# Identity transposes on TensorE during the first loads, a later place for pair 1's x transposes, and a later load of one block of the second weights, in a two-layer graph kernel

## The chip, the core and the metric

The kernel runs on one core of a Trainium2 chip. A core has five engines that run their own instruction streams and wait for each other through semaphores: TensorE (PE in the profile, with its weight loads as PEld), VectorE (DVE), ScalarE (ACT), GpSimd (POOL) and SyncE (SP). Transfers between HBM and on-chip memory are issued here from the queues of SP and ACT (SPq and ACTq) and carried by 16 DMA engines. The metric is the device time of one execution in microseconds (us); lower is better.

## The reference, cut to what matters

128 graphs of 128 nodes with 512 features each pass through two layers. In both, the result is added to the input and normalised over the features.

```python
# layer 0: attention over the neighbours, 8 heads of 64 units
feats = einsum('bnf,hfu->bhnu', X, W)
e_self, e_neigh = einsum('bhnu,hu->bhn', feats, a_self), einsum('bhnu,hu->bhn', feats, a_neigh)
dense = leaky_relu(e_self[..., :, None] + e_neigh[..., None, :], 0.2) + NEG_BIG * (1 - A)
out   = relu(einsum('bhij,bhju->bhiu', softmax(dense), feats) + b)
x = layernorm(x + out)

# layer 1: two hypergraph convolutions with a layer norm between them
H, w = (adj != 0), first row of adj
conv(x, W) = Dn * (H @ (Be * (H.T @ (x @ W.T)))) + bias      # Dn = 1/(H @ w), Be = 1/column sums of H
h = layer_norm(relu(conv(x, W1)), gamma, beta)
x = layernorm(x + conv(h, W2) + x)
```

## The kernel before

The graphs are taken in 64 pairs. Each pair runs through some ninety small steps: loads, transposes of x, features (a product with `w0_sb`), attention scores, masks, exponentials, transposes and weighted sums, the first normalisation, the propagator product, the hidden product with `w1_sb`, the output product with `w2_sb`, the last normalisation, the store. From pair 2 on, the products use sums of matrix blocks (seven products in place of eight), so that the weights need four extra sums of blocks each. Pairs 0 and 1 use plain products for the features (`plain_features`, lines 516 to 527) and transposes on TensorE in place of transposes on VectorE, because they run before everything else is ready.

The order of instructions is written out by hand. Every step has a time in a list (`todo`, lines 1140 to 1232): a step of pair p with lag l has the time (p + l) * 38.6 plus its own; the tables `todo` and `first` give special times for the start. The list is sorted by this time, and each engine's instructions are emitted in that order. The times are only keys for sorting: what runs when is decided by semaphores, and each engine and each DMA-issuing queue works strictly in its order. Line numbers below are those of the code before the change.

The steps of the start, in the order of their keys:

- Before the list: the input loads on SP and ACT (lines 177 to 189): the vectors `an_bc` and `as_bc`, four blocks of the first weights (`w0_raw`, `load_first`), x of pairs 0 and 1 (`load_rows`, line 120), adjacency rows. POOL writes the identity `ident` (line 206) that TensorE's transposes need.
- 11.1 and 12.0 `prepare_first` (line 228): for each of the four weight blocks a copy on ACT (L230), a product with `as_bc` on VectorE and with `an_bc` on POOL (L234), and two reductions on VectorE (L238). A block can be used by the features after its reductions.
- 11.4 `x_transpose_first` for pair 0 (line 393): eight transposes of x on TensorE into the banks `px` (L397). 11.5 `x_transpose_out`: two copies to `xT` on ACT (L405). `xT` has a single buffer, so that pair 1's copies wait until pair 0's features have been computed.
- 12.1 `load_weights` with `w2_blocks`: four loads of 512 KB of the second weights, issued on ACT's queue (L141).
- 12.5 `plain_features` 0 of pair 0, **12.55 `x_transpose_first` of pair 1**, 12.6 `plain_features` 1 of pair 0: TensorE (L523 and L397). A call of `plain_features` uses two weight blocks with four matmuls each, which the profile lists as eight records each.
- 12.65 `adj_transpose_first` (L410), 12.9 `nodes` (L360 to L369, VectorE), 13.0 `plain_features_out` (L533: copies of the features to `ft`, two on ACT and two on VectorE for pair 0), 13.05 `prepare_vectors`: one transpose on TensorE (L256) and its copy on ACT (L257), 13.1 the first copy to pair 1's `xT` on ACT.
- 13.5 `spread_rows` of pair 0: VectorE transposes `rows` (L542), and four small DMAs write them to `rd` in HBM, two issued by SP and two by ACT (L550). 13.8 the second copy to pair 1's `xT` on ACT.
- 14.0 `neighbours` of pair 0: two loads of 512 KB that spread `rd` to `nb`, one on SP and one on ACT (L570). 14.05 two blocks of the first hidden weights (`w1_blocks`) on ACT, and at 15.46 the other two on SP.
- 14.46 `edges`, 14.5 `plain_features` 0 of pair 1, 14.55 `propagator`, 14.6 `plain_features` 1 of pair 1, 16.0 `prepare_output` (lines 272 to 279: 32 matmuls `pv` over the four blocks of `w2_blocks`, in their order), then at 73 to 79 masks on POOL (L589), leaky ReLU on ACT (L605), maxima on VectorE (L611), exponentials on ACT (L619), the transposes `pet` on TensorE (L651), and the weighted sums `pav` (L677).

PSUM is used as eight banks of one pool: `bank(name)` takes the next, and a tile waits for the release of the one that had its bank.

Of the kernel before, what the change touches and what calls it, by code (L numbers as in the profile page):

```python
# [20 lines left out]
def kernel(  # L21
# [45 lines left out]
    nc = tc.nc  # L67
    G, N, F = x.shape
    P = 128
    DH = w1t.shape[1]  # L70
    H = 8
    U = F // H
    KF = F // P
    KH = DH // P
    HALF = 512
    QU = HALF // 2
# [12 lines left out]
    def bank(name):  # L89
        return psum.tile([P, HALF], F32, tag="bank", name=name)  # L90
# [95 lines left out]
    for i, ap in enumerate((gamma, beta, b1)):  # L186
# [7 lines left out]
    w2_blocks = ((w2_sb[:, 0, :, :QU], 0, 0), (w2_12, 0, 1), (w2_sb[:, 1, :, :QU], 1, 0),  # L194
                 (w2_sb[:, 2, :, :QU], 1, 1))
# [8 lines left out]

    ident = const.tile([P, P], F32, name="ident")
    make_identity(nc, ident)
    mhalf = const.tile([P, 2], F32, name="mhalf")
    nc.gpsimd.memset(mhalf, -0.5)

# [712 lines left out]
    def weigh(s, i, to, start):  # L922
# [3 lines left out]
          QU, 1, until=LAST)  # L926
# [197 lines left out]
    for t, fn, *args in (  # L1124
# [14 lines left out]
    T = 38.6  # L1139
    todo = [  # L1140
        (11.1, prepare_first, (0,)), (12.0, prepare_first, (1,)), (15.45, prepare_first_sums, ()),
        (12.1, load_weights, (nc.scalar, w2_blocks, w2t, DH // 2, QU)),
        (13.05, prepare_vectors, ()),
        (14.05, load_weights, (nc.scalar, w1_blocks[:2], w1t, F // 2, HALF)),
        (12.95, load_first_row, (1,)),
# [46 lines left out]

    for p, time, fn, *args in (
        (0, 11.4, x_transpose_first), (0, 11.5, x_transpose_out, 0), (0, 11.5, x_transpose_out, 1),
        (0, 12.5, plain_features, 0), (1, 12.55, x_transpose_first),
        (0, 12.6, plain_features, 1), (0, 12.65, adj_transpose_first),
        (0, 13.0, plain_features_out), (1, 13.1, x_transpose_out, 0), (1, 13.8, x_transpose_out, 1),
        (1, 14.5, plain_features, 0), (1, 14.6, plain_features, 1),
        (1, 15.6, plain_features_out), (1, 97.9, adj_transpose_first),
        (0, 78.8, e_transpose_first, 0, 0), (0, 78.85, e_transpose_first, 0, 1),  # L1200
        (0, 78.9, e_transpose_first, 1, 0), (0, 78.93, e_transpose_first, 1, 1),
    ):
        todo.append((time, run, (fn, p, args)))
# [74 lines left out]
```

## Time and profile before

| | |
|---|---|
| time, median of 3 runs | 2393.51 us (2392.73 to 2396.15) |
| profiled execution, its own time | 2398.11 us |
| its span, first to last instruction | 2396.3 us |
| TensorE busy | 2361.6 us (99%) |
| VectorE busy | 2087.9 us (87%) |
| GpSimd busy | 1823.2 us (76%) |
| ScalarE busy | 1528.2 us (64%) |
| mean granted TensorE clock | 0.997 |
| data moved by DMA | 347.09 MB, 145 GB/s in the mean |

Of an engine's line in the timeline, the first number is the start in us from the start of the span, the second the time in us from the first to the end of the last of the merged instructions, "xN" their count, and the bracket the engine's idle time before and what ended it. Times of matmuls are modelled at their ends, and consecutive ones overlap, so that the spacing of starts says more than a single duration. In the chain of waits each line is start, us and what the end of the program waited for at that time; "ACTq" and "SPq" are the queues that issue DMAs. A line that names a tile, as `nb<-rd`, says what is written from what.

### The profile page before, as it was taken

The page shows a single profiled execution, that of the slowest core. Times are in us where ns is not written, and L with a number is a line of the kernel's source. Part 1 is how long each engine was busy: PE and PEld are TensorE (multiplying, and loading weights), DVE is VectorE, ACT ScalarE, POOL GpSimd, SP SyncE. Part 2 cuts the span into 40 slices and gives each one's busy share as a digit, 9 for nine tenths or more (in the row PEclk, how much of TensorE's full clock was granted, in tenths as well). Part 3 has the DMA queues.
Part 4 walks back from the last instruction along what each step waited for, and adds up shares of the span by engine and source line. Part 5 has one row for each costly group of instructions (what it writes and reads, how often), then busy time and mean ns, then how long its engine had stood idle before and what let it go on. Part 6 is the DMA issues. An engine that isn't in the chain of part 4 may idle for free.

```text
span 2396.3 us, 80729 instructions
## 1 busy us (share of the span) xinstructions
PE 2361.6 (99%) x32309; PEld 1898.1 (79%) x32309; DVE 2087.9 (87%) x4456; ACT 1528.2 (64%) x4481; POOL 1823.2 (76%) x2060
## 2 busy tenths in 40 slices
PE   7999999999999999999999999999999999999998
PEld 6777777778778878778778788788888888788886
DVE  7988888888898898898888888988988988988875
ACT  4565765756667667667667566676676675676672
POOL 5877777777777877877877778778778778778774
PEclk9999999999999999999999999999999999999999
DMA  6555555555555555555555555555555555555541
GB/s 197 133 145 153 144 138 142 151 145 148 143 148 147 153 146 150 145 145 153 146 144 156 142 148 151 150 146 146 148 146 152 147 149 141 149 151 144 147 129 37
DMA packets 431134, 347.09 MB, mean 145 GB/s; under 512 B 151440, under 2 KB 380328, under 8 KB 430760
## 3 DMA queue, kind: packets, MB, share of 16 engines
q1 hardware_dynamic: 427288, 337.46, 50.1%
q8 instruction: 256, 4.19, 0.8%
q10 hardware_dynamic: 3472, 4.47, 0.6%
q14 instruction: 118, 0.97, 0.2%
HBM read 239.08 MB, written 102.73 MB: 143 GB/s over the span
## 4 chain that ended last, share of the span: by engine, by line
PE 81%; DMA 8%; DVE 4%; ACT 3%; POOL 2%; SPq 1%; issue 1%; DVEq 0%; POOLq 0%; ACTq 0%
PE phX L97 16%; PE pyX L97 15%; PE pfX L97 8%; PE phW L97 8%; PE pyW L97 7%; PE phY L97 4%; PE pfW L97 4%; PE pav L705 4%; PE pq L97 4%; PE pz L97 4%; PE pyY L97 4%; DMA ed<-nb 3%; DMA nb<-rd 2%; PE pfY L97 2%; ACT nb L605 1%; DMA rd<-rows 1%
## 5 line engine op out<-in xcount | busy, mean ns | idle before, releaser
L344 ACT COPY py<-pyX 128x257 f32<-128x257 f32 x189 | 70.6, 374 | 535.4 <-PE pyX L97 441.2
L97 PEld LDWEIGHTS phX<-zS,w_sb 128*64 128x64 f32 x6144 | 346.2, 137 | 37.8 <-POOL ft L744 23.4
L97 PE MATMUL phX<-zS,w_sb 128*64 128x128 f32 x6144 | 369.0, 273 | 2.6 <-ACT ph L344 2.6
L906 POOL TENSOR_TENSOR sq<-sq 128x512 f32<-128x512 f32 (+2 forms) x384 | 343.1, 894 | 20.1
L589 POOL TENSOR_TENSOR nb<-nb,neg 128x512 f32<-128x512 f32 x256 | 319.7, 1283 | 38.1 <-DMA nb<-rd 22.8
L605 ACT ACTIVATE nb<-nb,ft 128x128 f32<-128x128 f32 x1020 | 325.4, 392 | 21.8 <-POOL nb L589 21.7
L619 ACT ACTIVATE nb<-nb,nm 128x128 f32<-128x128 f32 x1024 | 319.2, 391 | 4.3 <-DVE nm L611 4.0
L769 POOL TENSOR_TENSOR rso<-veo,mhalf 128x2 f32<-128x2 f32 x63 | 44.1, 700 | 337.9 <-DVE veo L767 337.9
L97 PE MATMUL pyX<-w_sb,hS 128*64 128x257 f32 x2016 | 242.4, 381 | 0.0
L883 ACT ACTIVATE h<-h,vecs 128x128 f32<-128x128 f32 x768 | 240.5, 393 | 2.4 <-DVE h L868 1.4
L97 PE MATMUL pyX<-w_sb,h 128*64 128x257 f32 x2016 | 240.8, 379 | 0.5 <-ACT py L344 0.5
L97 PE MATMUL pyW<-w_sb,hS 128*64 128x256 f32 x2016 | 240.3, 379 | 0.1
L611 DVE TENSOR_REDUCE nm<-nb 128x4 f32<-128x512 f32 x256 | 175.3, 685 | 54.9 <-ACT nb L605 50.5
L744 POOL TENSOR_TENSOR ft<-ft,b_bc 128x512 f32<-128x512 f32 x128 | 203.9, 1613 | 6.2 <-ACT ft L533 6.2
L97 PEld LDWEIGHTS pyX<-w_sb,h 128*64 128x64 f32 x2016 | 149.8, 137 | 70.0 <-ACT py L344 0.9
L97 PEld LDWEIGHTS pyW<-w_sb,hS 128*64 128x64 f32 x2016 | 149.8, 137 | 69.2 <-issue 0.7
L97 PEld LDWEIGHTS pyX<-w_sb,hS 128*64 128x64 f32 x2016 | 144.7, 137 | 60.9
L640 DVE STREAM_TRANSPOSE eT<-eb 128x512 f32<-128x512 f32 x252 | 163.7, 686 | 12.0 <-DMA eb<-ed 11.1
L807 DVE SCALAR_TENSOR_TENSOR o<-y,b_bc 128x512 f32<-128x512 f32 x128 | 166.2, 1337 | 0.0
L1008 DVE SCALAR_TENSOR_TENSOR y<-y,rsh,bw_bc 128x512 f32<-128x512 f32 x126 | 150.2, 1230 | 16.3 <-POOL rsh L1004 16.3
L894 ACT ACTIVATE sq<-h 128x512 f32<-128x512 f32 x256 | 160.8, 629 | 2.1
L469 POOL TENSOR_TENSOR hS<-h 128x512 f32<-128x512 f32 x126 | 161.9, 1285 | 0.0
(178 smaller groups left out, 5568.1 us busy)
## 6 DMA issues: line engine op xcount, KB each, us to landing
nb<-rd SPq DMA_DIRECT2D x127, 512.0 KB, 6.0
ed<-nb SPq DMA_DIRECT2D x126, 512.0 KB, 3.6
eb<-ed SPq DMA_DIRECT2D x504, 128.0 KB, 2.9
x<-in_x_dram SPq DMA_DIRECT2D x64, 512.0 KB, 4.5
out_dram<-o SPq DMA_DIRECT2D x63, 512.0 KB, 2.9
xb<-in_x_dram SPq DMA_DIRECT2D x248, 128.0 KB, 5.5
a<-in_adj_dram SPq DMA_DIRECT2D x64, 128.0 KB, 2.3
w<-in_adj_dram SPq DMA_DIRECT2D x128, 64.0 KB, 5.1
```

What stands on the lines that cost most here:

```text
L97: nc.tensor.matmul(to[rows], lhs[:, rows], rhs, start=start, stop=stop, skip_group_check=True)
L469: engine.tensor_tensor(t[:, i], in0, in1, op=op)
L589: nc.gpsimd.tensor_tensor(t, t, neg[:, :, None, :].to_broadcast([P, NB, HH, B]), op=ALU.add)
L605: nc.scalar.activation(t, t, AF.Prelu, bias=s["ft"][:, g, h, 0:1], alpha=SLOPE)
L611: nc.vector.tensor_reduce(s["nm"][:, g, hs], scores(p, s, g, hs).rearrange("p b h j -> p h b j"), AX.XY, ALU.max, negate=True,)
L619: nc.scalar.activation(t, t, AF.Exp, bias=s["nm"][:, g, h:h + 1])
L640: nc.vector.transpose(s["eT"][:, g, hs, :].rearrange("p h (b i) -> p h b i", b=NB), s["eb", g][:, :, hs, :].rearrange("p b h j -> p h b j"),)
L744: nc.gpsimd.tensor_tensor(t, t, b0_bc.rearrange("p (h u) -> p h u", h=H), op=ALU.add)
L807: nc.vector.scalar_tensor_tensor(s["o"][:, g, :], s["y"][:, g, :], 2.0, b2_bc, op0=ALU.mult, op1=ALU.add)
L883: nc.scalar.activation(dst[:, k, :], src[:, k, :], AF.Relu, bias=b1_sb[:, c:c + 1])
L894: nc.scalar.activation(s["sq"][:, g, q * KH // 2:(q + 1) * KH // 2, :], hid(s, g, q), AF.Square, scale=DH ** -0.5,)
L906: nc.gpsimd.tensor_tensor(t[:, :n, :], t[:, :n, :], t[:, n:2 * n, :], op=ALU.add)
```

## The change

Three edits. After the identity is made, a bank `warm` is taken and TensorE transposes the identity into it 24 times; nothing reads the result. In the list, the four loads of the second weights become three at the old place, 12.1, and one, block (1, 1), at 14.04, which is after `neighbours` of pair 0 (14.0) and ahead of the first two blocks of `w1_blocks` (14.05) on ACT's queue. The eight transposes of pair 1's x move from 12.55 to 12.62, from between the two calls of `plain_features` of pair 0 to behind the second, ahead of `adj_transpose_first` (12.65).

```diff
     ident = const.tile([P, P], F32, name="ident")
     make_identity(nc, ident)
+    warm = bank("warm")
+    for i in range(24):
+        nc.tensor.transpose(warm[:, i % KF * N:(i % KF + 1) * N], ident, ident)
     mhalf = const.tile([P, 2], F32, name="mhalf")
...
         (11.1, prepare_first, (0,)), (12.0, prepare_first, (1,)), (15.45, prepare_first_sums, ()),
-        (12.1, load_weights, (nc.scalar, w2_blocks, w2t, DH // 2, QU)),
+        (12.1, load_weights, (nc.scalar, w2_blocks[:3], w2t, DH // 2, QU)),
+        (14.04, load_weights, (nc.scalar, w2_blocks[3:], w2t, DH // 2, QU)),
         (13.05, prepare_vectors, ()),
...
         (0, 11.4, x_transpose_first), (0, 11.5, x_transpose_out, 0), (0, 11.5, x_transpose_out, 1),
-        (0, 12.5, plain_features, 0), (1, 12.55, x_transpose_first),
+        (0, 12.5, plain_features, 0), (1, 12.62, x_transpose_first),
         (0, 12.6, plain_features, 1), (0, 12.65, adj_transpose_first),
```

## The prediction

> **What bounds the kernel now.** I read the busy shares first, then slices of the span, then the chain of waits, then the instructions of the first 40 us in order of time. The slices (columns: stretch, length, busy us and count of PE, PEld, DVE, ACT and POOL, granted clock, DMA share, GB/s) say where a change at the start can still count:
>
> ```profile
> 0.00:10.00 10.00, 1.95 (x9) 1.75 (x9) 3.12 (x4) 3.01 (x4) 3.70 (x15) 1.00 0.82 242
> 1600.00:2200.00 600.00, 600.00 (x8318) 498.55 (x8316) 534.59 (x1139) 394.23 (x1159) 467.04 (x525) 1.00 0.53 148
> ```
>
> TensorE (PE) works 1.95 of the first 10 us and all of the steady state. The change adds nothing to the steady state, so it moves the end by as much as it moves the moment from which PE never waits again. The chain (start, us, what) puts that moment near 131 us, and shows what leads to it at the start:
>
> ```profile
> 1.23 6.69 DMA x<-in_x_dram
> ...
> 8.05 1.96 PE px L397 x8
> 10.01 5.68 PE pf L523 x16
> 15.69 0.95 PE px L397 x8
> 16.64 3.58 PE pf L523 x16
> ...
> 21.45 0.43 ACTq L550
> ...
> 21.93 0.59 ACT xT L405
> ...
> 22.56 2.94 PE pf L523 x12
> ```
>
> ```profile
> 130.78 1.97 PE phX L97 x32
> ```
>
> The reader is to see that PE waits 8 us for x, that pair 1's transposes (15.69) stand between the halves of pair 0's features, and that the next features wait for an xT copy behind two DMA issues of ScalarE (ACT). The instructions in order of time (start, us, engine, line, operation) show the other gates:
>
> ```profile
> 10.59 1.28 DVE L238 TENSOR_REDUCE w<-wa 128x8 f32<-128x512 f32 x2
> 12.50 1.28 DVE L238 TENSOR_REDUCE w_sb<-wa 128x8 f32<-128x512 f32 x2
> 14.41 1.28 DVE L238 TENSOR_REDUCE w_sb<-wa 128x8 f32<-128x512 f32 x2
> 20.35 0.24 PE L256 MATMUL vecs_T<-ident,vec_rows 24*128 24x24 f32 x1
> 20.63 0.18 ACT L257 COPY vecs<-vecs_T 128x24 f32<-128x24 f32 x1 [0.90 <-PE vecs_T L256]
> 28.85 4.94 POOL L589 TENSOR_TENSOR nb<-nb,neg 128x512 f32<-128x512 f32 x4 [5.88 <-DMA nb<-rd]
> ```
>
> VectorE (DVE) finishes weight blocks 1, 2 and 3 at 11.87, 13.78 and 15.69; the features cannot pass these. From 20.35 to 39 two strands run side by side: vecs_T, ACT's copies and its half of the rd write, nb, masks, exponentials; and pair 1's features, then the 32 pv matmuls, to 36.8 on PE. They meet at the pet transposes.
>
> [...] the granted clock falls within 44 to 45 and returns within 51 to 52, an estimate of 6.8 us [...] from the shares 0.84 and 0.75:
>
> ```profile
> 44.00:45.00 1.00, 0.00 (x0) 0.00 (x0) 0.96 (x2) 0.05 (x1) 0.00 (x0) 0.84 0.95 316
> 51.00:52.00 1.00, 1.00 (x18) 1.00 (x16) 1.00 (x2) 0.79 (x3) 0.12 (x1) 0.75 0.03 4
> ```
>
> At the start the clock column reads 1.00, which the durations contradict: eight px records took 1.96 us at 8.05 and 1.12 at 15.53; eight pf records took 3.68 (9.84 to 13.52), sixteen later ones 3.56 (16.48 to 20.04). So PE is slow until about 13.9. [...] Here DMA is nearly idle from 21 to 24:
>
> ```profile
> 21.00:22.00 1.00, 0.65 (x3) 0.59 (x4) 0.96 (x6) 0.37 (x2) 1.00 (x1) 1.00 0.11 30
> 27.00:28.00 1.00, 1.00 (x6) 0.86 (x5) 0.49 (x2) 0.00 (x0) 0.00 (x0) 1.00 1.02 406
> ```
>
> **Part 1, 24 transposes of the identity.** ident is ready at 1.45 + 0.29 = 1.74. At the slow px rate of 0.22 (1.79 / 8 by starts) to 0.245 (1.96 / 8) they take 5.4 to 5.9 us and end at 7.1 to 7.6, before x at 8.05: hidden by the load. Their bank is the first of the rotation; every later bank moves by one, and only px of pair 1 now follows its release, by PE itself. Cost 0; with no cover it would be 5.9.
>
> If they lift the clock: px of pair 0 takes 1.12, but the first xT copy starts at 9.21 as before, since ACT copies a weight block from 8.68 to 9.31. Features start at 9.84 again. A fast pf record costs 3.56 / 16 = 0.2225, a group of eight 1.78. Group 1 ends at 11.62, group 2 starts at 11.87 (DVE) and ends at 13.65.
>
> **Part 2, pair 1's transposes behind pair 0's features.** Group 3 starts at 13.78 and ends at 15.56, group 4 from 15.69 to 17.47: against 20.04 before, 2.6 us sooner. The eight px of pair 1 move behind that: 0.95 us, to 18.42. The two adjacency transposes (0.31) bring vecs_T to 18.73, against 20.35: **1.6 us sooner**. On PE only adj and vecs_T stand behind the moved transposes, and ACT waits for vecs_T: its copy at 20.63, the xT copy, its two rd issues (21.05 to 21.88) and the second xT copy all move by 1.6. The DVE half of ft is done at about 18.1 and rows at 18.4, so SP's rd issues stop mattering; ACT's are the last, as now. The order of DMA issues on SP does not change.
>
> Pair 1's features move from 21.35 to 19.75, pv from 29.77 to 28.2. nb is issued at 22.2 for 23.8 and lands at 27.3 for 28.85, so masks, exponentials and pet follow by 1.6. From 39 to 62 the chain is DVE nearly without a gap, and beyond that chains of dependent work; I carry 1.6 to 131 us, and allow a loss of 0.6 on the way.
>
> **Part 3, the fourth block of w2 later.** The same instruction, 0.5 us of ACT's queue, goes from about 13.6 to behind ACT's nb issue at 24.2 (now 22.6). Behind it stand ACT's two w1 issues, then ACT's L605, which waits for POOL until 30.15: free. It takes 512 KB out of the busy stretch 14 to 20.5 (at some 320 GB/s 1.6 us), so that the rd writes, now 1.6 sooner, still meet an idle DMA. It adds 512 KB to the stretch 26 to 36: 1.3 us at 390 GB/s. Sharing with SP's first w1 block once nb is in, it lands by estimate at 27.3 + 1 MB / 390 GB/s = 30.0; the last eight pv matmuls need it at 35.0 - 1.6 = 33.4. Not late. w1_21 lands at 35.8 - 1.6 + 1.3 = 35.5; POOL's two hidden sums (2.37 each) end at 40.3, before the power at 45.5 - 1.6 = 43.9. SP's xb issues waited 1.7 us for w1's landing; they gain 0.3 instead of 1.6, and so does nb of pair 1 behind them (39.0 to about 38.5 at worst), whose mask runs only at 46.18.
>
> **Sum.** Removed from the path 1.6, added 0. The profiled execution takes 2398.1 (span 2396.3 and 1.8 around it), which would become 2396.5; it lies 4.6 above the median of the runs. So 2393.5 - 1.6 = **2391.9**. What bounds the unknown clock: with no lift 0; above, DVE's 15.69 stops any larger gain.
>
> **Rivals.**
> 1. *The transposes leave the clock slow.* [...] Then features run as now to 15.53, group 3 and 4 to 19.09, px of pair 1 to 20.04, where the adjacency transposes start today. The order of two pieces is exchanged and vecs_T stays at 20.35: gain 0, **2393.5**. A lift halfway gives a part, 0.24 us for each slow record saved.
> 2. *The gain is lost on the way to 131 us*, where SP's queue or the input loads keep their own time: also 2393.5, or part of it. For: the 1.3 us by which the loads end later. Against: the waits of 39 to 62 are on DVE.
> 3. *Slower: the moved w2 block is late for pv.* Place: PE's last eight pv matmuls, all pet behind them. It decides once the block lands after 35.0, and costs each us beyond it. If it lands only where w1_21 landed, 35.8, the time is 2393.5 + 0.8 = **2394.3**. Against: it stands second in ACT's queue, not third. For 0.2% it would have to land at 39.8, 16 us after its issue; the longest landing I see is 11.1.
>
> **Chances.** Forecast 0.52, rival 1 0.28, rival 2 0.10, rival 3 0.06, something unseen 0.04. Own range of the forecast: 2390.7 to 2393.1 (0.6 lost, or a little more than 1.6, and the run-to-run spread of a median, about 1). With rivals 1 and 2 the range is 2389.7 to 2394.8. A change of 0.2%, 4.8 us, is about what a measurement of this kernel can tell from none; no case reaches it by its own sum, since no single step moves by more than 2.6. Faster than that 0.04 (forecast plus spread), slower 0.04 (tail of rival 3 and the unseen), within 0.92.
>
> **What would show it.** Right: px at 8.05 takes about 1.1, the first eight pf records last 1.8 rather than 3.7, group 4 starts at DVE's 15.7, vecs_T near 18.7, nb masks near 27.3, pv ends near 35.2, the first unbroken PE stretch near 129.2. Rival 1: slow pf records up to about 14 and vecs_T at 20.3. Rival 2: vecs_T early, 131 us unchanged. Rival 3: PE idle between the 24th and 25th pv record. I would be wrong if the transposes outlast x's landing, if PE waits at pv, or if the steady state itself shows new waits.

## The result, and the profile after

| | before | after |
|---|---|---|
| median | 2393.44 us (2392.73 to 2397.39, 6 runs) | 2404.6 us (2398.94 to 2408.07, 6 runs) |
| span of the profiled execution | 2396.3 us | 2404.5 us |

The change makes the kernel slower: the medians are 11.2 us apart, and the ratio taken over the runs is 1.0039, 95% interval 1.0028 to 1.0049. The forecast was 2391.9 us and no change to be told from none.

**The start came out nearly as worked out.** Instructions of the changed kernel in order of time (start, us, engine, line, operation, tiles, count, idle before):

```profile
1.79 4.30 PE L209 MATMUL warm<-ident 128*128 128x128 f32 x24 [1.79 <-POOL ident masks.py:199]
...
7.86 1.23 PE L400 MATMUL px<-ident,x 128*128 128x128 f32 x8 [1.77 <-DMA x<-in_x_dram]
...
13.84 3.93 PE L526 MATMUL pf<-w_sb,xT 128*128 128x264 f32 x16
...
18.87 0.24 PE L259 MATMUL vecs_T<-ident,vec_rows 24*128 24x24 f32 x1
...
29.41 4.94 POOL L592 TENSOR_TENSOR nb<-nb,neg 128x512 f32<-128x512 f32 x4 [8.86 <-DMA nb<-rd]
```

The transposes are done at 6.1, px takes 1.23 us in place of 1.96, vecs_T comes at 18.87 in place of 20.35; but the masks on nb, which wait for its load, start at 29.41 in place of 28.85. The chain of waits of the changed kernel (start, us, what) shows how little of the gain is left in this execution:

```profile
16.89 3.72 DMA dd_d<-dr
...
20.64 0.32 ACTq L553
...
21.00 0.59 ACT xT L408
...
28.92 7.01 PE pv L279 x32
35.93 1.22 PE pet L654 x8
...
37.16 2.33 PE pet L654 x8
```

```profile
130.17 1.97 PE phX L97 x32
```

The second rd issue of ScalarE's queue waited, as the profile puts it, for the small dd_d write, so the xT copy behind it is only 0.93 us sooner (21.00, was 21.93), and TensorE's pet transposes stop in the middle for the late masks. At the place where I had put the end of all waiting, the product phX starts at 130.17 instead of 130.78: **0.6 us sooner, in a kernel that ends 8.2 us later** (2404.5 less 2396.3). The loss lies behind this point.

**The steady state.** Slices of the span (stretch, length, busy us and count of PE, PEld, DVE, ACT, POOL, clock, DMA share, GB/s), first of the kernel before, then of the changed one:

```profile
135.00:700.00 565.00, 559.00 (x7724) 443.47 (x7722) 494.03 (x1055) 366.33 (x1079) 431.87 (x487) 1.00 0.53 147
700.00:1550.00 850.00, 849.89 (x11762) 671.42 (x11760) 753.22 (x1612) 552.59 (x1623) 663.75 (x746) 1.00 0.52 147
```

```profile
135.00:700.00 565.00, 561.21 (x7746) 448.44 (x7744) 493.95 (x1061) 368.90 (x1085) 431.71 (x489) 1.00 0.53 146
700.00:1550.00 850.00, 842.18 (x11608) 666.34 (x11606) 741.11 (x1590) 548.08 (x1612) 652.74 (x738) 1.00 0.52 146
1600.00:2200.00 600.00, 600.00 (x8356) 476.11 (x8354) 529.79 (x1137) 397.51 (x1171) 467.85 (x530) 1.00 0.53 148
```

The kernel before loses 6 us of TensorE up to 700 and nothing after; the changed kernel goes on losing (7.8 us) from 700 to 1550, and nothing from 1600 to 2200. Taken from the starts of the first pz product of each pair, a pair lasts 36.37 us in the good stretches. In the kernel before, slow pairs (36.4 to 38 us) end with pair 17; in the changed one with pair 39. From pair 3 to pair 61, the time above 36.37 a pair adds up to 9.5 us before and 18.6 after; this sum is called the excess below. The waits of TensorE from 135 to 2300 (waiter, releaser: us, times, longest), first before, then after, and the shares of the chain by engine, in the same order:

```profile
PE phX L97 <- ACT zT L831: 4.7, 7, 1.5
PE pav L705 <- DVE eT L640: 1.1, 3, 0.5
```

```profile
PE phX L97 <- ACT zT L834: 9.3, 15, 1.1
PE pav L708 <- DVE eT L643: 1.8, 5, 0.7
```

```profile
PE 81%; DMA 8%; DVE 4%; ACT 3%; POOL 2%; SPq 1%; issue 1%; DVEq 0%; POOLq 0%; ACTq 0%
```

```profile
PE 58%; DMA 21%; DVE 6%; ACT 6%; POOL 4%; SPq 3%; issue 2%; DVEq 0%; POOLq 0%; ACTq 0%
```

The end of the changed kernel hangs on DMA for 21% of the span. A stretch of its chain shows which:

```profile
1110.87 2.69 DMA rd<-rows
...
1113.58 4.78 DMA nb<-rd
...
1119.71 1.29 POOL nb L592
...
1128.76 5.98 DMA ed<-nb
```

In the 29 slow pairs of the changed kernel (pairs 3 to 60), nb was issued 2.5 us after rd (16 KB) in the median, and the first read-back from ed 5.9 us after its write; in the 29 others it was 1.5 and 3.5. The load of nb waits for rd, and SP's queue behind it; masks, exponentials and zT on ScalarE follow late, and TensorE waits at phX. It waits for other engines' results, not for its own instructions: the two entries, 11.1 us, are nearly all of its idle time from 135 to 2200 (11.6 us).

### The profile page after: what moved, and what is told of

Its sections match the earlier page's. It is cut to its first block, busy times and chain, and to the rows that moved or that the text cites. A ratio compares the mean times of both kernels' runs of the same rounds, so it can differ in the third digit from the quotient of the medians.

```text
span 2404.5 us, 80776 instructions
## 1 busy us (share of the span) xinstructions
PE 2368.7 (99%) x32333; PEld 1876.3 (78%) x32333; DVE 2079.0 (86%) x4456; ACT 1527.7 (64%) x4481; POOL 1821.0 (76%) x2060
## 4 chain that ended last, share of the span: by engine, by line
PE 58%; DMA 21%; DVE 6%; ACT 6%; POOL 4%; SPq 3%; issue 2%; DVEq 0%; POOLq 0%; ACTq 0%
PE phX L97 12%; PE pyX L97 10%; DMA ed<-nb 9%; DMA nb<-rd 6%; PE pfX L97 6%; PE phW L97 5%; PE pyW L97 5%; PE phY L97 3%; DMA rd<-rows 3%; ACT nb L608 3%; PE pfW L97 3%; PE pq L97 3%; DMA eb<-ed 3%; PE pav L708 3%; PE pz L97 3%; PE pyY L97 2%
## 5 line engine op out<-in xcount | busy, mean ns | idle before, releaser
L97 PEld LDWEIGHTS pyW<-w_sb,hS 128*64 128x64 f32 x2016 | 144.9, 136 | 73.9 <-issue 1.3
```

Source lines behind the costliest of these rows:

```text
L97: nc.tensor.matmul(to[rows], lhs[:, rows], rhs, start=start, stop=stop, skip_group_check=True)
```

## The experiments

Each run was timed beside the kernel before on the same chip, whose median was 2392.01 us in the first four, 2391.88 in the next four, 2393.28 and 2391.47 in the last two pairs.

### The three edits, each alone

Three theories stood at first: A, the pairs have a slow and a fast rhythm, and the timing of the start decides by chance which one is entered; B, the bank that the transposes take shifts the rotation of the PSUM banks in every later pair; C, the moved w2 load delays the queues for good.

`warm_only` adds the 24 transposes, `order_only` moves the transposes of pair 1's x, `w2_only` moves the fourth w2 block:

```diff
+    warm = bank("warm")
+    for i in range(24):
+        nc.tensor.transpose(warm[:, i % KF * N:(i % KF + 1) * N], ident, ident)
```

```diff
-        (0, 12.5, plain_features, 0), (1, 12.55, x_transpose_first),
+        (0, 12.5, plain_features, 0), (1, 12.62, x_transpose_first),
```

```diff
-        (12.1, load_weights, (nc.scalar, w2_blocks, w2t, DH // 2, QU)),
+        (12.1, load_weights, (nc.scalar, w2_blocks[:3], w2t, DH // 2, QU)),
+        (14.04, load_weights, (nc.scalar, w2_blocks[3:], w2t, DH // 2, QU)),
```

> Before plus the 24 identity transposes alone. Theory A (two rhythms: the steady state falls into a slow rhythm of 36.4 to 38 us a pair, in which nb is asked for about 8 us ahead of pz and SP's transfers collide, and leaves it for a fast one of 36.37 by chance of timing; the change only alters the timing with which it is entered): pair 3 begins within 1 us of before's 165.0, the sum of the slow pairs is another than before's 9 us, total anywhere from 2388 to 2408; no part has a price of its own. Theory B (every PSUM bank moves by one, which costs in each pair): total about 2404 as after. Theory C (the later w2 load alone does it): total 2393, as before.

> Before with pair 1's x transposes at 12.62 alone. Theory A: pair 3 begins within 1 us of 165.0, total anywhere from 2388 to 2408, by the number of slow pairs. Theory B: no bank moves, 2393. Theory C: 2393.

> Before with the fourth w2 block at 14.04 alone. Theory A: pair 3 begins within 1 us of 165.0, total anywhere from 2388 to 2408. Theory B: 2393. Theory C: about 2404, as after.

Measured: warm_only 2398.02 us, ratio 1.0029 (1.0019 to 1.0038); order_only 2392.73, 1.0002 (0.9994 to 1.001); w2_only 2393.83, 1.0006 (0.9998 to 1.0014). So the w2 load is not the cause, nor the moved transposes: the 24 transposes, which are done at 6.1 us and which nobody waits for, cost most of the loss (1.0029 of 1.0039). Slow pairs end at about pair 38 in warm_only, 13 in order_only, 16 in w2_only.

### One more delay of TensorE

`after_kick` is the changed kernel with 32 more transposes ahead of pz of pair 4, which should push TensorE behind the queues once.

```diff
         t = s["pz", g] = bank(f"pz_{p}_{g}")
+        if (p, g) == (4, 0):
+            for _ in range(32):
+                nc.tensor.transpose(t[:, :N], ident, ident)
```

> After plus 32 identity transposes on TensorE in front of pz of pair 4, about 3.8 us of added work, once, in pz's own bank. Theory A: one large delay of TensorE lets the SP queue get ahead, nb of the next pair is asked for 9.6 us ahead of pz, and the fast rhythm sets in at pair 5 rather than 40: after's 18 us of slow pairs shrink to about 1, so 2404.6 + 3.8 - 17 = about 2391; work added makes it faster. Theory B or C: 2404.6 + 3.8 = 2408.

Measured: 2401.36 us, ratio 1.004 (1.0027 to 1.0053), which none of the theories had forecast. The nb load of pair 4 was issued 12.0 us ahead of pz, as wanted; at pair 5 it was back to 8.4, and the pairs stayed slow to the very end. A rhythm that one delay would set for good (theory A) falls. Shifted banks (theory B) fit no better: the slow pairs end at 17, 39 and never, with nothing in the banks to end them.

### What counts: TensorE's instructions, by 256

The queues of the changed kernel, in the profile's table (packets, MB, share of 16 engines):

```profile
q8 instruction: 256, 4.19, 0.8%
```

These are 256 packets of 16,384 bytes, each about 1 us long (0.9 to 2.1). TensorE has 65,537 records in the kernel before, 256 for each of its 256 packets. They follow the count of records: in the changed kernel each starts 157 to 342 records behind a multiple of 256. So I take one packet for a fetch: the transfer of one block of TensorE's instructions. (The other engines have 15,192 records; beside q8 stand 118 packets of 8,192 bytes on another instruction queue, q14.) In the steady state a pair has 1022 TensorE instructions, two less than four blocks, so the four fetches of a pair drift later against the pair's work by two instructions a pair. In slow pairs one fetch lies inside the rd write, within about 1.2 us of its issue; in the fast stretch it has drifted behind it, to 1.3 us and more (rd 11.26 us ahead of pz, the fetch 9.9 and less). The 24 transposes are 48 instructions: every fetch falls 48 instructions earlier in the pairs' work, and 48 / 2 = 24 pairs more are needed: from pair 17 to about 40. The 64 instructions of after_kick add 32 pairs, beyond the last. This is theory D. It says that *more* unused instructions, up to just short of 256, should make the kernel faster than both.

Four kernels, with unused instructions in stretches in which TensorE waits (a tiny product is counted as four, since the trace lists the four matmuls on a weight block in `plain_features` as eight matmul and eight weight-load records): 226 or 256 in all, on the kernel before and on the changed one. For `before_226`:

```diff
+    warm = bank("warm")
+    for _ in range(30):
+        nc.tensor.matmul(warm[:2, :2], mhalf, mhalf, start=True, stop=True)
...
         t = s["pz", g] = bank(f"pz_{p}_{g}")
+        if (p, g) == (0, 0):
+            for _ in range(26):
+                nc.tensor.matmul(t[:2, :2], mhalf, mhalf, start=True, stop=True)
+            for _ in range(1):
+                nc.tensor.transpose(t[:, :N], ident, ident)
```

`before_256` has 34, 30 and 0 of them; `after_226` 12, 32 and 1; `after_256` 16, 36 and 0, beside the 24 transposes.

> Kernel before plus 226 unused TensorE instructions ahead of the first weighted sums (tiny 2-column products of a constant, and one identity transpose, in stretches where TensorE waits anyway). Theory D: TensorE's instruction fetch, 16 KB or 256 instructions a piece, drifts by 2 instructions a pair (1022 used, 1024 fetched) against the small rd and ed writes; while a piece falls into those writes a pair takes 0.2 to 0.9 us longer than 36.37. 226 is 30 short of 256, so the pieces come 15 pairs later in their drift: slow pairs end at about pair 2 or 3 in place of 17; the 9 us of slow pairs go: 2384 to 2386, if nothing comes back in the last pairs. Theory B (any work added ahead on TensorE, or a moved bank, brings in a slow rhythm): 2398 as with the 24 transposes, or more, since 226 is nearly five times 48.

> As the one with 226, but 256 unused TensorE instructions, which is one whole piece of the fetch. Theory D: every piece boundary in the steady state falls where it fell before: slow pairs to about pair 17, 2392 to 2393.5. Theory B: 2398 or more, slow pairs to 39 or beyond.

> The changed kernel plus 178 unused TensorE instructions, which makes 226 with the 48 of its 24 transposes. Theory D: slow pairs end at about pair 2 or 3, 2384 to 2386, about 18 us below the changed kernel and 7 below the kernel before. Theory B: no gain, 2402 to 2408.

> The changed kernel plus 208 unused TensorE instructions, 256 with its own 48. Theory D: slow pairs to about pair 17 as in the kernel before, so the time shows what the change is worth by itself at an equal fetch phase: 2392 to 2393.5. Theory B: 2402 to 2408. Had the three edits themselves a cost in the steady state (the moved w2 block, the moved transposes), it would stay here: 2396 or more.

| | median, us | ratio to before (95%) | slow pairs until about | excess, pairs 3 to 61, us | rd writes with a fetch in them, of 58 |
|---|---|---|---|---|---|
| before (+0) | 2393.44 | | 17 | 9.5 | 13 |
| changed (+48) | 2404.6 | 1.0039 (1.0028 to 1.0049) | 39 | 18.6 | 36 |
| after_kick (+48, +64) | 2401.36 | 1.004 (1.0027 to 1.0053) | the end | 14.8, of which 3.7 are the 32 transposes | 55 |
| before_226 | 2388.38 | 0.9983 (0.9977 to 0.999) | 3 | 0.4 | 2 |
| before_256 | 2392.26 | 1.0002 (0.9994 to 1.001) | 16 | 6.5 | 12 |
| after_226 | 2388.69 | 0.9986 (0.9979 to 0.9992) | 3 | 0.5 | 5 |
| after_256 | 2393.54 | 1.0005 (0.9997 to 1.0013) | 17 | 8.8 | 15 |

(Excess: first pz of pair 61 less that of pair 3, less 58 times 36.37. The last column takes the rd writes ahead of pz of pairs 0 to 57, and counts those with a fetch under way between 0.3 and 1.25 us after the issue. All from one profiled execution each, the medians from the runs.)

With 256 the loss of the changed kernel is gone, though all three edits are in it; with 226 it beats the kernel before. Theory B expected 2398 and more for all four, and falls: all four have the added bank. The size of the gain was put too high (2384 to 2386 expected): I had taken the 9 us of the one profiled execution of before, where before_256 and the two harmless single edits show 5.5 to 6.7. The first slice again, and the only wait of TensorE at phX, in before_226:

```profile
135.00:700.00 565.00, 565.00 (x7850) 470.30 (x7848) 503.33 (x1070) 370.37 (x1089) 439.86 (x494) 1.00 0.52 149
```

```profile
PE phX L97 <- ACT zT L839: 0.2, 1, 0.2
```

In 565 us TensorE is busy for 565: that is what the prediction had taken for granted of the kernel before.

### The drift stopped

If the drift ends the slow pairs, stopping it must keep them. A 2 x 2 transpose in each pair from pair 2 on should bring 1022 to 1024; the unused instructions at the start (240 or 200) choose where the fetches stand.

```diff
+        if p >= 2 and g == 0:
+            nc.tensor.transpose(t[:2, :2], ident[:2, :2], ident[:2, :2])
         for k in range(KF):
```

> Kernel before plus 240 unused TensorE instructions at the start, and from pair 2 on one 2 x 2 transpose (two instructions) a pair, so that a pair has 1024 instructions, four whole pieces, and the drift stops. 240 is 16 short of 256: the pieces stand for good where the kernel before has them in its pair 10, in the rd and ed writes. Theory D: all pairs slow, 0.5 to 1.0 us each over 62 pairs, so 31 to 62 us more than lock_fast. Theory B or A (the rhythm is set by the start, the drift means nothing): within 5 us of lock_fast, since the two differ in ten tiny products at the start alone.

> As lock_slow, with 200 unused instructions at the start in place of 240: the pieces stand where the kernel before has them in its pair 30. Theory D: all pairs fast; 2386 to 2388 plus what the 62 added transposes take on TensorE (0.03 to 0.1 us each by estimate, 2 to 6 us): 2388 to 2394. Theory B or A: about the same as lock_slow.

Measured: lock_slow 2406.44 us (ratio 1.0055, 1.004 to 1.0069), lock_fast 2402.93 (1.0042, 1.0027 to 1.0056). They are 3.5 us apart, where theory D wanted 31 or more, and the pair decides nothing. The trace gives the reason: 1023 instructions a pair, since one of twelve separate semaphore instructions on TensorE had become needless. The fetches still drifted, at half the speed, and had left the rd write by pair 13; in lock_slow pairs from 10 on last 36.61 us like those of lock_fast. So the transpose went behind the first matmul of pz, where it takes over no wait:

```diff
             )
+            if p >= 2 and (g, k) == (0, 0):
+                nc.tensor.transpose(t[:2, N:N + 2], ident[:2, :2], ident[:2, :2])
```

> lock_slow mended. Its trace has 1023 instructions a pair and not 1024, since the added transpose made one of the twelve separate semaphore instructions of line 97 needless; so its drift was halved and not stopped, and its slow pairs ended at about pair 13. Here the 2 x 2 transpose stands behind the first matmul of pz, where it takes over no wait, for 1024; 244 unused instructions at the start hold the pieces 16 instructions ahead of where the kernel before starts. Theory D: no end to the slow pairs, 36.9 to 37.2 each where hold_fast has about 36.6 (what lock_slow's pairs 3 to 8 and its later pairs show), so 19 to 37 us above hold_fast. Theory A or B: within 5 us of hold_fast.

> As hold_slow with 200 unused instructions at the start: the pieces are held where the kernel before has them in its pair 30. Theory D: 36.6 each from pair 4 to the end, about 2402 as lock_fast (62 times 0.24 us of TensorE above 2388). Theory A or B: as hold_slow.

Measured: hold_slow 2416.21 us (2413.39 to 2419.13; ratio 1.01, 1.0084 to 1.0115), hold_fast 2402.29 (2400.93 to 2403.28; 1.0045, 1.0032 to 1.0058). The two differ in 44 unused instructions at the start, and by 13.9 us. In hold_slow the fetch stays at 9.8 to 10.6 us ahead of pz from pair 3 to pair 61, slow pairs occur to the end, and the fetch lies in 56 of 58 rd writes; in hold_fast in 1. The moment at which the steady state starts is not what differs: pz of pair 3 comes at 166.82 us in hold_slow and in after_226, which is fast. The chain's shares, first of hold_slow, then of hold_fast:

```profile
PE 65%; DMA 16%; POOL 5%; DVE 5%; ACT 4%; SPq 2%; issue 2%; DVEq 0%; POOLq 0%
```

```profile
PE 94%; DVE 2%; DMA 2%; ACT 1%; issue 0%; POOL 0%; SPq 0%; DVEq 0%; POOLq 0%; ACTq 0%
```

The direction is theory D's, the size less than its 19 to 37 us: its pairs lasted 36.86 in the mean, 0.25 above 36.61. Only 31 of the 57 pairs with a fetch in the rd write (pairs 3 to 60) were slow, though nb was as late in the others (3.0 us after rd in the median of both). A likely part of the reason, not tried: the added transpose slows every pair by 0.24 us (0.03 to 0.1 had been expected), and so gives the late chain as much more room.

### Inside one rd write

SP's queue in pair 33 of hold_slow, then in pair 18 of hold_fast (start, us, queue, line, what); nb waits for rd:

```profile
1262.27 0.40 SPq L555 DMA_DIRECT2D rd<-rows  x1
1265.33 0.39 SPq L573 DMA_DIRECT2D nb<-rd  x1
```

```profile
702.30 0.34 SPq L555 DMA_DIRECT2D rd<-rows  x1
703.74 1.39 SPq L573 DMA_DIRECT2D nb<-rd  x2
```

DMA in the stretch between the two issues; 40 equal slices, busy tenths of the 16 engines, then packets by queue. First pair 33 of hold_slow, 1262.30 to 1265.30, a slice being 0.075 us:

```profile
DMA  3688300488926410000000000000000000000000
GB/s 63 104 137 133 50 10 7 75 147 132 285 38 99 65 14 0 0 0 0 0 0 0 0 0 0 3 5 5 0 0 0 0 0 0 0 0 0 0 0 0
...
q1 hardware_dynamic: 729, 0.09, 18.7%
q8 instruction: 1, 0.02, 2.3%
```

Then pair 18 of hold_fast, 702.30 to 703.74, a slice being 0.036 us:

```profile
DMA  4697864211001358987530037864200090000000
...
q1 hardware_dynamic: 674, 0.08, 35.4%
```

In both, nearly all of rd's packets are through 1.1 us after the issue. In the slow pair a few stray ones (3 to 5 GB/s) come at 1.9 us. Packet by packet, in us from the rd issue: the fetch of 16,384 bytes lasts from 0.84 to 1.97; eight packets of 128 bytes and one of 4 run from 1.95 to 2.14. The profile does not say which engine carries a packet. Where no other packets of its queue run beside such a write, as at 706.10 us in the changed kernel, the trace lists 128 packets of 128 bytes and 16 of 4 for it; an even share of 16 engines would be eight and one, so that by my estimate the late ones are one engine's share. In the kernel before, 9 of the 13 writes with a fetch in them end in the same way: eight packets of 128 bytes and one of 4, the first of which starts within the last 0.02 us of the fetch. So the last nine packets of a 16 KB write came when the fetch ended, and nb is issued 3.06 us after rd in place of 1.44. Of these 1.6 us, 1.07 is the later end of the last packet (2.14 against 1.07); the rest passes between the last packet and the issue of nb, 0.92 here and 0.37 in the fast pair, and the profile doesn't explain it. That the nine packets waited for the fetch on the same engine is read from these times; the trace records no such wait.

Over 58 rd writes of the changed kernel (those of the table): in 34 of the 36 with a fetch in them, nb was issued over 2 us after rd (2.46 in the median), and in 4 of the 22 others (1.53).

## Why the prediction was wrong

- **The step that failed** is this sentence: "The change adds nothing to the steady state, so it moves the end by as much as it moves the moment from which PE never waits again." The 24 transposes add 48 instructions ahead of the steady state and move every later 256-instruction fetch against the pairs' work: the stretch with slow pairs is 22 pairs longer and the excess 9 us larger, where the sum had 0. The chance for "something unseen" was 0.04; of the signs of being wrong that the prediction had named, the one that came is new waits in the steady state. The second half of the sentence was off for the kernel before as well: behind 131 us its TensorE still waited some 6 us, up to pair 17. The profile of before shows it: the prediction rests on the slice 1600 to 2200 and on the chain at 131, while from 200 to 400 TensorE was busy for 198.07 of 200 us and from 400 to 800 for 395.93 of 400, and the waits at phX add up to 4.7 us.
- **Part 1, cost 0** held for the place and failed for the program. The transposes ended at 6.1, ahead of x, and delayed nothing around them; but alone they cost 1.0029. That they cost anything is an accident of the position: 226 instructions gain (0.9983 in before_226), 256 change nothing (1.0002 in before_256).
- **The clock.** Rival 1 falls: with the transposes the clock rose sooner. The trace's record of the granted clock has it full from 4.8 us, 3 us after the first transpose (13.96 before); px took 1.23 us. In the five traces with the 24 transposes it is full from 4.8 to 7.8 us on, in the nine without from 11.9 to 14.2; in one of the five, after_226, it fell to half again from 9.9 to 13.3. What sets these moments was not shown.
- **Part 2.** vecs_T at 18.87 was forecast at 18.73, group 4 bound by VectorE as worked out. What was off in this execution is what 1.6 us becomes on the way: nb was issued 1.0 sooner, not 1.6, and landed in 6.6 us instead of 5.05, so that the masks came 0.56 later; pv started 0.93 sooner; 0.6 was left at 131. Rival 2 thus took a good half of the gain here. It is one execution: in after_kick, the same program up to pair 4, the masks came at 27.52, close to the forecast 27.3, and phX at 128.49, 2.3 sooner than before. The slow landing is not the price of the w2 block behind it: with the same block, nb's masks came 4.9 to 5.0 us after the issue in after_kick, after_226 and after_256, and 4.8 in w2_only.
- **Part 3** was right: pv ran its 32 products in 7.01 us as before. Rival 3 falls.
- **What the change is worth by itself,** at an equal fetch position: after_256 less before_256 is +1.3 us, after_226 less before_226 +0.3, both within the spread of the runs. The 1.6 us of gain doesn't show; the first pz came at 46.7 to 49.5 us in the four kernels with all three edits and at 47.1 to 49.9 in the seven without any.
- **Open.** That the position of the fetches decides, and that a fetch in the rd write makes nb late, is shown. What a late nb costs is not: the excess of the pairs with a fetch in the rd write (pairs 3 to 60), divided by their number, is 0.65 us in before, 0.48 in the changed kernel, 0.25 in warm_only and hold_slow, and 0.20 in after_kick without its 32 transposes. In before_226 a fetch comes back into the rd write from pair 57 on, with nb 2.7 to 3.0 us behind rd, and pairs 57 to 60 take 36.5 us at most. So a late nb alone is not enough for a slow pair. For the two ed writes of a pair, 5.9 us in place of 3.5 for the first, I only have that two fetches fall into them in 27 of the 29 slow pairs of the changed kernel and in 9 of the 29 others; loads that slide into them because SP's queue is late may have as large a share. hold_slow and hold_fast differ there too (57 of 58 pairs, and none), so that the shares of rd and ed aren't separated. It wasn't tried. The waits at pav, for the transposes of what is read back from ed, are the smaller part of TensorE's idle time (1.8 of 11.1 us).

## What to carry to other kernels

Before you trust "added where the engine waits, so free", count the instructions it adds: in this long unrolled program 48 of them shifted every later instruction fetch against the work of the pairs, and with a 16 KB write on the way to TensorE's next product the time rose by a ratio of 1.0029 (warm_only). When an edit far from the loss moves the time, compare the period of each loop round over the whole span, not a sample of it, and look whether slow rounds begin or end at a round that moves with the count of instructions. A cheap test is to add one whole block of unused instructions (256 here) and then some 30 less: here the first changed nothing (1.0002), and the second told what the position is worth (3.9 us, 2392.26 to 2388.38).

## What the runs showed of the hardware

- A fetch of TensorE's instructions is one packet of 16,384 bytes, 0.9 to 2.1 us long in the changed kernel. In the pair shown, with such a fetch from 0.84 to 1.97 us after the issue of a 16 KB write, the last nine packets of the write ran from 1.95 to 2.14; in the pair without one the last ended at 1.07. The dependent issue came at 3.06 in place of 1.44.
- 44 unused instructions at the start of a program of some 65,900 moved it by 13.9 us (2402.29 to 2416.21).
- One 2 x 2 float32 transpose in each pair cost 0.24 us a pair (36.61 instead of 36.37), though its own record is 0.16 us long.
- With 24 float32 transposes of 128x128 from 1.8 us on, the recorded clock was full from 4.8 to 7.8 us on (five traces), without them from 11.9 to 14.2 (nine).
